# Buffers, stage places and PSUM banks in the scan part of a decoder layer: three decay half-sets, a gate every four chunks, three places a step

## The chip, the core and the metric

The kernel runs on one core of one Trainium2 chip. The metric is device time in microseconds, from the start to the end of one launch; a time is a median of several runs. Five engines work beside each other, each with its own queue of instructions: TensorE (PE in the profile; PEld is its weight load), VectorE (DVE), ScalarE (ACT), GpSimd (POOL) and SyncE (SP), which here only starts DMAs.

## The reference

The layer takes x and a context, both 8 x 256 x 256 (batch, sequence, width), and does three things in turn, each followed by a residual sum and a layernorm without gain.

A Mamba block: a projection to 2 x 512 channels, a causal convolution over 4 positions with silu, projections to a step size (softplus), B and C, and then the recurrence over 256 positions with 16 states for each of the 512 channels:

```
h = h * exp(d_t * A) + (d_t * u_t) * b_t
y = sum over the 16 states of h * c_t
y = (y + u * D_param) * silu(z)
out = y @ out_proj_w.T
```

A cross attention of one head to the context (keys and values are the same), whose result is normed and given to a feed-forward part of width 1024 with relu, and normed again.

A mixture of experts: 160 experts, the 8 best of each token by sigmoid, each expert a silu layer of width 128, and one shared expert.

## The kernel before

The program has a front (the Mamba block, the attention, the feed-forward part and the routing) and a back (the experts, from L768 on). The change is in the front only.

The front's recurrence goes over 128 steps: 8 batches b of 16 chunks n. A chunk is 32 channels by 16 states, laid on 128 partitions (32 channels by 4 states) and NG = 4 groups of 256 positions. One step n does this:

- `product` (L375): GpSimd multiplies the rows of B with step size times u into g, 128 x 1024. It is made LEAD = 3 steps ahead.
- `decays` (L381): ScalarE makes exp(d * A), 4 activations of 256 positions, into `decay`, two tiles of two groups in PSUM. They are written for the next step, behind the scans that read them.
- `scans` (L388): VectorE runs the recurrence as two scans of 2 x 256, one for each half-set.
- `read_out` (L397): VectorE multiplies the states with the rows of C into h.
- every fourth step `summed` (L412): TensorE adds up 16 states for 4 chunks into `ya`, 32 matmuls.

Beside this run two chains, Python generators that hand out one stage at each `yield`. `head(b + 1)` (L261) makes projections, convolution, silu, step size and the DMAs that spread them, for the next batch. `rest(b - 1)` (L423) does the previous batch's out projection, norm, attention, feed-forward part, norms and routing up to the places of its tokens; `scatter` (L660) then writes these to a table by indirect DMAs. `go` (L671) runs the first chain of a list to its next yield. For TensorE, VectorE, ScalarE and GpSimd the order in which the program issues instructions is the order of their queues (`manual_schedule`, L682), so an instruction that waits holds up all that stands behind it on its engine. SP's order is left to the planner.

In the kernel before, rest and head each get a stage in the middle of a step (behind the decays) and one at its end (behind read_out). If two rests are in the list, up to two more stages of the first are run at each of these. Head begins at n = 2 and is run to its end at n = NC - 6 = 10. Rest begins at the end of n = 0 of the next batch. Its second stage multiplies all of `ya` with silu(z) (L434), and needs `ya` of the whole batch, two PSUM tiles. `skipped` (L403) starts `ya` with u * D_param at n = 2.

The other matmuls of rest and head write to one pool of two PSUM tiles in turn (`bank`, L133; `ps_front`). A tile is given again when its readers are done.

When the last step is done, what is left of rest 6 and all of rest 7 run alone: the tail. Then come the counts of tokens, the gathering of token blocks and the experts' blocks.

Names that the steps of the prediction use: pj and pz (L266, L292) are the head's projections, L285 the convolution, L303 and L304 the silus, px and pd the projections to step size, L333 to L347 the softplus; po (L437), pk, pv and pq (L464, L472, L484), psc (L492), pat and pm (L517, L527) are the attention's banks; L538 makes x2, x2t (L546) is its turned form, ph and pf (L556, L568) are the feed-forward matmuls with relu (L567) between them, L576 adds their sum; L603 is the sigmoid, L613 the search for the 8 best, L638 to L644 the places, L650 to L656 the weights.

Of the kernel before, what the change touches and what calls it, by code (L numbers as in the profile page):

```python
# [9 lines left out]
F32 = mybir.dt.float32  # L10
AF = mybir.ActivationFunctionType
# [56 lines left out]
def decoder_layer(  # L68
# [109 lines left out]
    with ExitStack() as first:  # L178
# [3 lines left out]
        m3 = first.enter_context(tc.tile_pool(name="m3", bufs=PAIRS))  # L182
        m4 = first.enter_context(tc.tile_pool(name="m4", bufs=4))
        m5 = first.enter_context(tc.tile_pool(name="m5", bufs=5))
        pools["ps"] = first.enter_context(tc.tile_pool(name="ps_front", bufs=2, space=PSUM))
        acc = first.enter_context(tc.tile_pool(name="acc_front", bufs=2, space=PSUM))
# [64 lines left out]
        decay = [held.tile([P, 2, S], F32, name=f"decay{j}") for j in range(NG // 2)]  # L251
# [3 lines left out]
        states_f = states.rearrange("p g t -> p (g t)")  # L255

# [4 lines left out]
        def head(b, made):  # L261

            u = m1.tile([P, KI, S], F32, tag="u", name=f"u_{b}")
            sz = m2.tile([P, KI, S], F32, tag="sz", name=f"sz_{b}")
            for j in range(KI // 2):
                pj = bank(f"pj_{b}_{j}").rearrange("p (e t) -> p e t", e=2)  # L266
                for e in range(2):
                    o = (2 * j + e) * P
                    for k in range(KD):
                        nc.tensor.matmul(  # L270
                            pj[:, e, :], in_x[:, k, o : o + P], xt[:, k, :], start=(k == 0), stop=(k == KD - 1)
                        )
                yield
# [7 lines left out]
                for e in range(2):  # L281
                    k = 2 * j + e
                    for i in range(NTAP - 1):
# [5 lines left out]
                    if e == 0:  # L289
                        yield  # L290
            for j in range(KI // 2):
                pz = bank(f"pz_{b}_{j}").rearrange("p (e t) -> p e t", e=2)  # L292
                for e in range(2):
                    o = (2 * j + e) * P
                    for k in range(KD):
                        nc.tensor.matmul(
                            pz[:, e, :], in_z[:, k, o : o + P], xt[:, k, :], start=(k == 0), stop=(k == KD - 1)
                        )
                yield
                nc.scalar.copy(sz[:, 2 * j : 2 * j + 2, :], pz)  # L300
# [4 lines left out]
            exps()  # L305
            px = bank(f"px_{b}")
# [31 lines left out]
            yield  # L338
            nc.vector.scalar_tensor_tensor(e, delta, 1.0, e, ALU.subtract, ALU.subtract)
# [3 lines left out]
            exps()  # L343
            nc.gpsimd.tensor_sub(delta, delta, e)
            yield
# [16 lines left out]
        def spread(b, j, made):  # L362

            both = []
            for a, name in enumerate(("spread_delta", "spread_du")):
                t = m3.tile([P, 2, S], F32, tag=name, name=f"{name}_{b}_{j}")
# [14 lines left out]
        def decays(b, n, made):  # L381
            delta = made["spread"][n // 2][0]
            for g in range(NG):
                nc.scalar.activation(  # L384
                    decay[g // 2][:, g % 2, 1:], delta[:, n % 2, 1:], AF.Exp, scale=na[:, n * NG + g : n * NG + g + 1]
                )

        def scans(b, n, made):  # L388

            gf = made.pop(n)  # L390
            for j in range(NG // 2):
                part = slice(j * NT, (j + 1) * NT)
                nc.vector.tensor_tensor_scan(  # L393
                    states_f[:, part], decay[j].rearrange("p g t -> p (g t)"), gf[:, part], 0.0, ALU.mult, ALU.add
                )
# [7 lines left out]
        def skipped(b, made):  # L403

            made["ya"] = [acc.tile([P, NT], F32, tag="acc", name=f"ya_{b}_{j}") for j in range(KI // 2)]
            for k in range(KI):
                nc.tensor.matmul(
                    made["ya"][k // 2][:, (k % 2) * S : (k % 2 + 1) * S], diag[:, k, :], made["u"][:, k, :],
                    start=(k % 2 == 0), stop=False, skip_group_check=True,
                )  # L410

        def summed(b, k, made):  # L412


            hs = [made.pop(("h", k * NR + q)) for q in range(NR)]
            for g in range(NG):
                for q in range(NR):
                    nc.tensor.matmul(  # L418
                        made["ya"][k // 2][q * CH : (q + 1) * CH, (k % 2) * S : (k % 2 + 1) * S], over, hs[q][:, g, :],
# [3 lines left out]
        def rest(b, sz, ya):  # L423
# [7 lines left out]
            yield  # L431
            for j in range(KI // 2):
                g = sz[:, 2 * j : 2 * j + 2, :].rearrange("p k t -> p (k t)")
                nc.vector.tensor_mul(g, g, ya[j])  # L434
            yield

            po = bank(f"po_{b}").rearrange("p (c d) -> p c d", c=TT)  # L437
            for c in range(TT):
                for k in range(KI):
# [3 lines left out]
                    )  # L443
            yield
# [18 lines left out]

            pk = projected(wk, ct, "kt")  # L464
            yield
            nc.vector.tensor_add(xn, xn, po)
            kt = biased(early[:, 0], pk, C_BK)
            x1 = a1.tile([P, TT, D], F32, tag="x1", name=f"x1_{b}")
            layernorm(x1, xn, f"x1_{b}")
# [9 lines left out]
            nc.scalar.copy(val, pv)  # L479
            pt = turned(x1, f"x1_{b}")  # L480
            yield
            x1t = a1.tile([P, KD, S], F32, tag="x1t", name=f"x1t_{b}")
            nc.scalar.copy(x1t, pt)
            pq = projected(wq, x1t, "qt")  # L484
            yield
            qt = biased(early[:, 1], pq, C_BQ)
# [4 lines left out]
            nc.gpsimd.tensor_add(x1, x1, mid(rv[:, R_H2 : R_H2 + D], TT))  # L491
# [578 lines left out]
```

## Time and profile before

| | us |
| --- | --- |
| median of 11 runs | 1540.67 |
| lowest, highest | 1539.25, 1546.86 |
| the profiled execution | 1543.89 |
| its span, first to last instruction | 1542.2 |
| first scan | 51.62 |
| 128 steps | 51.6 to 850 |
| tail of the front | 850 to 943 |
| the rest, experts included | 943 to 1542.2 |
| mean granted TensorE clock | 0.803 |

A group's line gives busy time, the mean of one, and the idle time of its engine just before it with what ended that. A wait's line gives the total, how often, and the longest. A stretch's line gives its bounds and length, the busy time of PE, PEld, DVE, ACT and POOL with the number of instructions, the granted clock of TensorE, the DMA engines' share and GB/s. An order-of-time line gives start, length, engine, line, operation, operands and the count that was merged, with the idle time before it in brackets. The largest groups of the steps, of one step each: a scan of 128 x 512 1.229 us (L393), a product 2.354 (L378), one decay activation 0.474 (L384), a read_out 1.220 (L400). GpSimd's and VectorE's other work lies between these.

### The profile page before, as it was taken

How to read it: one execution, taken by the hardware profiler on the slowest of the kernel's cores; microseconds unless marked ns; L12 is line 12 of the kernel's file. 1: busy time of each engine (PE TensorE's matmuls, PEld its weight loads, DVE VectorE, ACT ScalarE, POOL GpSimd, SP SyncE). 2: the span in 40 equal slices, each digit the busy share in tenths (PEclk: the TensorE clock that was granted, in tenths of full speed). 3: DMA queues.
4: the chain of work that ended last, by engine and by line, in shares of the span. 5: the costliest groups of instructions: out<-in, count | busy, mean ns of one | idle time of the engine just before them, and what ended most of it. 6: DMA issues, size and time to landing. Idle time of an engine off the chain costs nothing. (4 is left out here: it accounts for less than half of the span.)

```text
span 1542.2 us, 18276 instructions
## 1 busy us (share of the span) xinstructions
PE 1004.5 (65%) x4831; PEld 703.3 (46%) x4831; DVE 880.0 (57%) x1776; ACT 667.6 (43%) x1540; POOL 883.0 (57%) x713
## 2 busy tenths in 40 slices
PE   4345757667657657575666661078888888877675
PEld 3223435345434534453444441056666666644333
DVE  2578778778768777887888317089433333310000
ACT  4264664854846647748546230022222222212222
POOL 1546374775756657747766014565656666637775
PEclk8576876878869868768778875579999999987877
DMA  6334752242343332323320000066867788634443
GB/s 206 109 95 121 236 176 64 53 108 50 56 96 63 65 83 61 101 64 48 110 53 2 21 7 7 3 190 198 239 198 219 212 228 249 196 115 132 132 133 93
DMA packets 159985, 177.13 MB, mean 115 GB/s; under 512 B 29220, under 2 KB 135238, under 8 KB 159872
## 3 DMA queue, kind: packets, MB, share of 16 engines
q1 hardware_dynamic: 127360, 131.31, 30.8%
q0 software_dynamic: 20704, 33.81, 8.3%
q10 hardware_dynamic: 11808, 10.75, 2.1%
q8 instruction: 42, 0.69, 0.2%
q14 instruction: 71, 0.58, 0.2%
HBM read 160.54 MB, written 51.97 MB: 138 GB/s over the span
## 5 line engine op out<-in xcount | busy, mean ns | idle before, releaser
L378 POOL TENSOR_TENSOR g<-bc,spread_du 128x1024 f32<-128x1024 f32 x128 | 300.2, 2354 | 118.2 <-DVE states L393 72.8
L393 DVE TENSOR_TENSOR_SCAN states<-decay,g 128x512 f32<-128x512 f32 x256 | 314.5, 1229 | 63.0 <-ACT decay L384 30.5
L384 ACT ACTIVATE decay<-spread_delta,na 128x255 f32<-128x255 f32 x512 | 238.5, 474 | 183.3 <-DVE states L393 153.2
L884 POOL DMA_INDIRECT xg<-x_d,tokens x216 | 215.9, 999 | 131.7 <-PE bt L895 122.1
L897 DVE COPY bx<-bt 128x256 f32<-128x256 f32 x216 | 91.5, 423 | 180.2 <-PE bt L895 178.4
L906 PE MATMUL by<-we,bg 128*128 128x256 f32 x432 | 151.4, 433 | 43.7 <-ACT bg L904 36.0
L904 ACT ACTIVATE bg<-bh 128x128 f32<-128x128 f32 x216 | 60.0, 278 | 246.9 <-PE bh L900 246.7
L400 DVE TENSOR_TENSOR h<-states,bc 128x1024 f32<-128x1024 f32 x128 | 156.1, 1220 | 9.5 <-PE ya L418 3.8
L988 POOL DMA_INDIRECT y<-y_d,sloti x128 | 121.0, 946 | 58.2 <-issue 55.1
L664 POOL DMA_INDIRECT tab_d<-pair_no,placei x128 | 125.7, 982 | 46.0 <-issue 30.2
L900 PEld LDWEIGHTS bh<-bx,we 128*128 128x128 f32 x864 | 129.9, 193 | 20.5 <-DVE bx L897 8.1
L900 PE MATMUL bh<-bx,we 128*128 128x128 f32 x864 | 134.6, 279 | 4.3 <-DVE bx L897 2.8
L994 PE MATMUL yn<-y,diags 128*128 128x256 f32 x256 | 108.1, 537 | 43.8 <-DMA y<-y_d,sloti 43.0
L906 PEld LDWEIGHTS by<-we,bg 128*128 128x128 f32 x432 | 65.4, 189 | 95.9 <-ACT bg L904 95.4
L418 PE MATMUL ya<-h,over 128*32 128x256 f32 x1024 | 87.6, 466 | 30.2 <-DVE h L400 30.2
L560 PE MATMUL ph<-x2t,w_sb 128*128 128x256 f32 x256 | 73.7, 458 | 47.8 <-ACT x2t L548 47.8
L171 PE MATMUL pt_x<-ident,x 128*128 128x128 f32 x96 | 26.4, 381 | 115.0 <-ACT x L162 99.1
L994 PEld LDWEIGHTS yn<-y,diags 128*128 128x128 f32 x256 | 55.8, 253 | 94.2 <-DMA y<-y_d,sloti 88.8
L995 DVE TENSOR_TENSOR xs<-xs,yn 128x512 f32<-128x512 f32 x8 | 5.5, 688 | 157.4 <-PE yn L994 157.4
L560 PEld LDWEIGHTS ph<-x2t,w_sb 128*128 128x128 f32 x256 | 59.5, 236 | 61.3 <-ACT x2t L548 50.4
L895 PE MATMUL bt<-ident,xg 128*128 128x128 f32 x432 | 83.6, 275 | 3.7 <-DMA xg<-x_d,tokens 3.7
L171 PEld LDWEIGHTS pt_x<-ident,x 128*128 128x128 f32 x96 | 14.0, 178 | 130.3 <-ACT x L162 111.5
(224 smaller groups left out, 1734.7 us busy)
## 6 DMA issues: line engine op xcount, KB each, us to landing
we<-in_experts_dram SPq DMA_DIRECT2D x216, 256.0 KB, 4.7
y_d<-bo SPq DMA_DIRECT2D x216, 128.0 KB, 3.2
spread_delta<-spread_d SPq DMA_DIRECT2D x256, 64.0 KB, 2.1
spread_du<-spread_d SPq DMA_DIRECT2D x256, 64.0 KB, 1.9
y_d<-none ACTq DMA_DIRECT2D x1, 9216.0 KB
bc<-bc_d SPq DMA_DIRECT2D x64, 128.0 KB, 4.7
spread_d<-delta SPq DMA_DIRECT2D x8, 512.0 KB
spread_d<-v SPq DMA_DIRECT2D x8, 512.0 KB
```

What stands on the lines that cost most here:

```text
L378: nc.gpsimd.tensor_mul(g, made["bc"][0], mid(made["spread"][n // 2][1][:, n % 2, :], NG))
L384: nc.scalar.activation(decay[g // 2][:, g % 2, 1:], delta[:, n % 2, 1:], AF.Exp, scale=na[:, n * NG + g : n * NG + g + 1])
L393: nc.vector.tensor_tensor_scan(states_f[:, part], decay[j].rearrange("p g t -> p (g t)"), gf[:, part], 0.0, ALU.mult, ALU.add)
L400: nc.vector.tensor_mul(h, states, made["bc"][1])
L560: nc.tensor.matmul(ph[:, i, :], w1_sb[:, k, f * P : (f + 1) * P], x2t[:, k, :], start=(k == 0), stop=(k == KD - 1),)
L664: nc.gpsimd.indirect_dma_start(out=tab_views[i * TOPK + j], out_offset=bass.IndirectOffsetOnAxis(ap=placei[:, c, j : j + 1], axis=0), in_= ...
L884: nc.gpsimd.indirect_dma_start(out=xg[i % LANES], out_offset=None, in_=x3_d, in_offset=bass.IndirectOffsetOnAxis(ap=tokens[:, i : i + 1], ...
L897: nc.vector.tensor_copy(xt, pt)
L900: nc.tensor.matmul(ph, w[:, k * P : (k + 1) * P], xt[:, k * P : (k + 1) * P], start=(k == 0), stop=(k == KD - 1))
L906: nc.tensor.matmul(py, g, w[:, KD * P :], start=True, stop=True)
L988: nc.gpsimd.indirect_dma_start(out=y8[:, j, :], out_offset=None, in_=y_d, in_offset=bass.IndirectOffsetOnAxis(ap=sloti[:, i, j : j + 1], a ...
L994: nc.tensor.matmul(pn[:, c, :], diags[:, i, j, :], y8[:, j, :], start=False, stop=(j == TOPK - 1))
```

## The change

- `decay` becomes three tiles (half-sets) instead of two; half-set j of step i uses tile (2 i + j) mod 3. `decays` and `scans` are called for one half-set. The first half for step i + 1 is written ahead of step i's scans, the second half behind them.
- A step has three places for rest: between the scans, behind the second scan (and the decays), behind read_out. With two rests in the list a place runs two stages. Head gets a stage at the second and third place, and one between the scans at even n.
- `ya` is one held PSUM tile of two 256-wide halves. `summed` begins a half with the product of u and D_param itself, and `gated` multiplies it with silu(z) one step later, at n = 1, 5, 9, 13. `skipped` is gone. Rest begins with po, at the last place of n = 1, and its three loads (`fetched`) are issued at n = 0.
- Rest and head have one PSUM tile each (`ps_rest`, `ps_head`) instead of two shared ones.
- Head begins at n = 0; the run to its end stands at the start of n = 10.
- More yields lie between an instruction and those that need its result, in rest and head. In rest, the norm of x1 comes ahead of pk.
- u has two buffers instead of one, silu(z) three instead of two; the g buffers stay four, under another name of the pool.

```diff
-        m3 = first.enter_context(tc.tile_pool(name="m3", bufs=PAIRS))
-        m4 = first.enter_context(tc.tile_pool(name="m4", bufs=4))
+        m3 = first.enter_context(tc.tile_pool(name="m3", bufs=3))
+        m4 = first.enter_context(tc.tile_pool(name="m4", bufs=PAIRS))
-        pools["ps"] = first.enter_context(tc.tile_pool(name="ps_front", bufs=2, space=PSUM))
-        acc = first.enter_context(tc.tile_pool(name="acc_front", bufs=2, space=PSUM))
+        pools["ps"] = first.enter_context(tc.tile_pool(name="ps_rest", bufs=1, space=PSUM))
+        ps_head = first.enter_context(tc.tile_pool(name="ps_head", bufs=1, space=PSUM))
...
-        decay = [held.tile([P, 2, S], F32, name=f"decay{j}") for j in range(NG // 2)]
+        decay = [held.tile([P, NG // 2, S], F32, name=f"decay{j}") for j in range(3)]
+        ya = held.tile([P, 2, S], F32, name="ya")
...
-            u = m1.tile([P, KI, S], F32, tag="u", name=f"u_{b}")
-            sz = m2.tile([P, KI, S], F32, tag="sz", name=f"sz_{b}")
+            u = m2.tile([P, KI, S], F32, tag="u", name=f"u_{b}")
+            sz = m3.tile([P, KI, S], F32, tag="sz", name=f"sz_{b}")
...
                 for e in range(2):
                     k = 2 * j + e
+                    yield
                     for i in range(NTAP - 1):
...
-                    if e == 0:
-                        yield
...
             exps()
+            yield
             px = bank(f"px_{b}")
...
             nc.scalar.activation(delta, delta, AF.Ln)
             exps()
+            yield
             nc.gpsimd.tensor_sub(delta, delta, e)
+            yield
             yield
             yield
...
-        def decays(b, n, made):
+        def decays(i, b, n, made, j):
+
             delta = made["spread"][n // 2][0]
-            for g in range(NG):
+            for e in range(NG // 2):
+                g = j * (NG // 2) + e
                 nc.scalar.activation(
-                    decay[g // 2][:, g % 2, 1:], delta[:, n % 2, 1:], AF.Exp, scale=na[:, n * NG + g : n * NG + g + 1]
+                    decay[(2 * i + j) % 3][:, e, 1:], delta[:, n % 2, 1:], AF.Exp,
+                    scale=na[:, n * NG + g : n * NG + g + 1],
                 )
...
         def summed(b, k, made):
+            nc.tensor.matmul(
+                ya[:, k % 2, :], diag[:, k, :], made["u"][:, k, :], start=True, stop=False, skip_group_check=True
+            )
...
-        def rest(b, sz, ya):
+        def gated(k, made):
+            nc.vector.tensor_mul(made["sz"][:, k, :], made["sz"][:, k, :], ya[:, k % 2, :])
+
+        def fetched(b):
...
+            return xn, ct, cn
+
+        def rest(b, sz, xn, ct, cn):
...
             yield
+            yield
...
-            pk = projected(wk, ct, "kt")
-            yield
             nc.vector.tensor_add(xn, xn, po)
-            kt = biased(early[:, 0], pk, C_BK)
             x1 = a1.tile([P, TT, D], F32, tag="x1", name=f"x1_{b}")
             layernorm(x1, xn, f"x1_{b}")
+            yield
+            pk = projected(wk, ct, "kt")
+            yield
+            yield
+            kt = biased(early[:, 0], pk, C_BK)
...
                     nc.scalar.activation(ht[:, f, :], ph[:, i, :], AF.Relu, bias=cv[:, C_B1 + f : C_B1 + f + 1])
+            yield
             pf = bank(f"pf_{b}").rearrange("p (c d) -> p c d", c=TT)
...
             for i, (b, n) in enumerate(steps):
...
-                scans(b, n, made)
+                if n == 0:
+                    if b + 1 < B:
+                        heads.append(head(b + 1, rows_made[b + 1]))
+                    if b > 0:
+                        begins = fetched(b - 1)
+                if n == 10:
+                    while heads:
+                        go(heads)
+                if after:
+                    decays(i + 1, *steps[i + 1], after_made, 0)
+                scans(i, b, n, made, 0)
                 while ahead < min(i + LEAD + 1, len(steps)) and ahead // 2 < loaded:
                     product(*steps[ahead], rows_made[steps[ahead][0]])
                     ahead += 1
-                if i + 1 < len(steps):
-                    decays(*steps[i + 1], rows_made[steps[i + 1][0]])
-                go(rests)
-                for _ in range(2):
-                    if len(rests) > 1:
-                        go(rests)
...
+                beside(rests)
+                if n % 2 == 0:
+                    go(heads)
+                scans(i, b, n, made, 1)
+                if after:
+                    decays(i + 1, *steps[i + 1], after_made, 1)
+                beside(rests)
+
                 if n % NR == 0 and i > 0:
                     b0, n0 = steps[i - 1]
                     summed(b0, n0 // NR, rows_made[b0])
                 go(heads)
                 read_out(b, n, made)
...
+                made.pop(n)
+                if n % NR == 1 and i > 1:
+                    b0, n0 = steps[i - 2]
+                    gated(n0 // NR, rows_made[b0])
+                    if n == 1:
+                        rests.append(rest(b0, rows_made[b0]["sz"], *begins))
+                beside(rests)
                 go(heads)
...
                 go(scattered)
```

`beside` runs one stage of the first rest, and a second one if two are in the list.

## The prediction

> **What bounds the kernel now.** I read the page first (busy shares and the 40 slices), then the stretches, then VectorE's waits, then the order of time of one batch.
>
> ```profile
> PE 1004.5 (65%) x4831; PEld 703.3 (46%) x4831; DVE 880.0 (57%) x1776; ACT 667.6 (43%) x1540; POOL 883.0 (57%) x713
> ...
> DVE  2578778778768777887888317089433333310000
> ACT  4264664854846647748546230022222222212222
> ```
>
> No engine is full. In slices 2 to 22, where the 128 scan steps run, VectorE is the fullest; the change touches only this part and what comes just before and after it. The stretches of five like batches, of the last batch, of the tail behind the last step, and of the rest:
>
> ```profile
> 234.80:763.80 529.00, 343.71 (x1740) 243.29 (x1740) 411.65 (x576) 332.33 (x711) 337.38 (x216) 0.78 0.33 73
> 759.80:850.00 90.20, 60.45 (x307) 42.04 (x311) 73.93 (x102) 50.01 (x120) 54.17 (x38) 0.75 0.15 37
> 850.00:943.00 93.00, 53.79 (x215) 39.52 (x212) 29.43 (x138) 25.66 (x62) 18.01 (x27) 0.74 0.05 14
> 943.00:1542.20 599.20, 429.12 (x2041) 303.64 (x2041) 209.18 (x785) 130.97 (x402) 365.90 (x374) 0.86 0.56 163
> ```
>
> 529.0 / 5 = 105.8 us a batch, of which VectorE (third pair) works 82.3. Some 4 us are the gaps between its instructions, so about 19 us a batch are waits. They are spread over many causes:
>
> ```profile
> DVE states L393 <- ACT decay L384: 30.5, 16, 3.6
> DVE best L613 <- ACT pr L603: 21.2, 7, 5.9
> DVE e L339 <- ACT delta L336: 15.2, 7, 2.5
> DVE delta L347 <- POOL delta L344: 13.3, 7, 4.2
> ...
> DVE x L576 <- PE pf L571: 11.3, 7, 2.3
> DVE den L628 <- ACT den L620: 10.6, 7, 1.7
> ```
>
> All of them over the 128 steps (without 11.8 at the start) are about 142 us: the most that the change can take away. A step with nothing else is short: scans at 635.26 and at 639.29, 4.0 us apart.
>
> ```profile
> 635.26 2.57 DVE L393 TENSOR_TENSOR_SCAN states<-decay,g 128x512 f32<-128x512 f32 x2
> 637.94 1.23 DVE L400 TENSOR_TENSOR h<-states,bc 128x1024 f32<-128x1024 f32 x1
> 639.29 2.57 DVE L393 TENSOR_TENSOR_SCAN states<-decay,g 128x512 f32<-128x512 f32 x2
> 643.39 0.69 DVE L576 TENSOR_TENSOR x<-x,pf 128x512 f32<-128x512 f32 x1 [1.53 <-PE pf L571]
> ```
>
> The last line is the join that will matter: VectorE reaches the FFN's sum and waits 1.53 for TensorE, which had been busy with it since 627.23:
>
> ```profile
> 627.23 8.93 PE L560 MATMUL ph<-x2t,w_sb 128*128 128x256 f32 x32 [7.25 <-ACT x2t L548]
> 636.18 7.17 PE L571 MATMUL pf<-w_sb,ht 128*128 128x256 f32 x32
> 643.28 1.93 PE L418 MATMUL ya<-h,over 128*32 128x256 f32 x32
> ```
>
> **Where the stages come to stand.** Counting yields, rest grows from 39 stages to 51, head from 17 to 23. With three places a step (A between the scans, B behind the second, C behind read_out), from the third batch on: xn's sum stands at step 2 C, x2's at 9 B, x2t at 10 B, ph 0 to 3 at 10 C to 11 C, pf's halves at 12 B and 12 C, the FFN's sum at 13 B, sigmoid at 16 A (step 0 of the next batch), the top 8 at 1 A, places and weights at 2 A. The head: convolutions at steps 1 to 3, the two silus at 4 between the scans, exp at 6, the logarithm at 7, the end at 8.
>
> **What goes.** decays for a first half waits for a scan one and a half steps back, so the plain decay wait goes. sigmoid has a whole step before the top 8 (-3.0 a batch, 21.2 / 7), den, exp and u get distance (-1.5, -2.2, -1.4).
>
> **What comes.** I follow one batch round: VectorE, then ScalarE, then TensorE, each handing over to the next.
>
> Segment 1, VectorE, from the FFN's sum (13 B) to the last convolution (step 3): 0.7 + 1.05 (norm statistics) + 1.25 (read_out) + 0.45 (a gate of 256; the 256-wide sum at L693 took 0.42) = 3.45; step 14 is 4.0 + 1.05 + 0.4 wait for POOL's two sums; steps 15 and 0 are 4.0 each; step 1 is 4.0 + 2.2 (top 8) + 0.2 + 3.0 (two convolutions of 1.5) + 0.45; step 2 is 4.0 + 3.0 (places, 2.5 to 3.6 in the trace) + 1.9 (weights) + 1.75 + 1.5; step 3 up to its convolution is 2.6 + 1.5. Sum 43.0.
>
> Segment 2. The head has one bank, so pz waits for the last convolution: 2.0, copy 0.6, second pz 2.0, copy 0.6, hops 0.1: 5.3. Then ScalarE is nearly without a pause up to x2t: table, silu, silu, table 4.7; 13 half-sets of decays at 0.95 (two of 0.474) = 12.4; x1t, val, xd, prob_t and at 2.8; v twice and qt 2.6; abs, exp and the 1+ 3.3; top and softmax 1.5; logarithm with two tables 3.7; x2's norm 2.1; x2t 1.0: 34.1 in all, with about 5 of waits, of which 2.9 is for x2's sum that waits for pm. With the 5.3: 44.4. Inside it VectorE meets the second half-set of step 5, which stands behind the silus: from the last convolution to that decay's end 5.3 + 4.7 + 0.95 = 11, VectorE needs 1.25 + 4.0 + 1.3 = 6.5: a wait of 4.5 in place of the 3.6 seen now. At steps 7 and 9 it waits another 2 and 1.4.
>
> Segment 3. After x2t the first ph takes 3.75 (the trace has 627.23 to 631.02, granted clock 0.52 up to 631 and 1.00 after); with one bank each next ph waits for the relu before: 3 x 1.75, and 4 x (0.84 + hops) = 3.6; pf's halves 3.6 each; summed, which now stands between them with its own diagonal product, 1.93 + 0.47. Sum 22.2, where before the same stretch took 16.1. VectorE has 0.65 of step 10, steps 11 and 12 and two scans to do: 11.2. So it waits 11 us, partly for step 13's decays behind the relus.
>
> Round: 43.0 + 44.4 + 22.2 = 109.6, 3.8 more than 105.8. Both ends: the first ph at full clock -2, half of ScalarE's 5 us of waits gone -2.5: 105.1; pz at the low clock, as at 84.59 where it took 3.65, +1.65, and 2 for VectorE and POOL slowing each other (L640 has a mean of 1.2 against 0.17 alone): 113. I take 109.6, since the last batch and the tail show ph after a pause at the low clock each time.
>
> The other parts: batches 2 to 6, 5 x 3.8 = +19. Batch 1 (95.3 now) has no top 8, places or weights; by the same round without 4.1 + 3.0 of these it comes to 102: +6.5. Batch 0 (83.9): 8.6 for the first step, 77 for the rest with a 4.5 to 6 wait at the silus: +2. Batch 7 (90.2), where the head is missing but segment 3 is whole: 91, +1. The first head runs alone: its second pj and first pz wait for convolutions instead of a second bank, 20.0 to 26.5 at the silus' start, +6.5. The tail: po no longer waits for the places (-5.5), but pk and pv share a bank (+4.2) and so do the ph (+3.5): +2. Asking for xn, ct and cn a step earlier costs nothing: 0.4 us each on SP's queue, which stands idle from 571.9 to 576.35 in the batch read here. The head's DMAs move two steps forward with it, so the next batch's spreads are asked for at step 10 instead of 11; VectorE waits for no DMA in a steady batch, so this hides behind four pairs loaded ahead, and without these it would cost up to the 2 us that one transfer takes. On POOL steps 7 to 9 now hold three products, the head's two products and three scatters, 3 x 2.36 + 2 x 2.35 + 3 x 2.5 = 19.3 against some 19 of VectorE's; the three products made ahead cover it, and without them each us beyond would be VectorE's. The experts' part (599 us) is not touched. Sum +37. The profiled execution took 1543.89, its span 1542.2 and 1.7 around it; the median is 3.2 lower. I put the sum on the median: 1540.7 + 37 = **1578**.
>
> **Two rules of the Trainium skill.** On one bank instead of two, the trace has relus 1.73 apart with two banks, and 1.75 + 0.9 is the round with one. "TensorE: Matmul & The Clock Gate", section "HAM oscillation", tells of a kernel in which a second PSUM buffer gave no further gain; by it the second bank's loss would cost nothing, 2.7 a batch less, and the sum would be about 1559; no run here has shown it yet, and that kernel had no relu between.
> The trace has a silu starting 0.01 us after its 1.28 us table (601.42, 602.71). "ScalarE: Activation LUTs", section "What ACT_TABLE_LOAD costs", adds a drain of about 1.38 to each load; by it the silus would hold ScalarE 2.8 longer in each of 7 batches and the sum would be near 1597. The row decides.
>
> **Rivals.**
> (a) Slower, as summed: 1553 to 1600 (the ends of the round over five batches, 3 us for the rest). Chance 0.50.
> (b) Faster: the FFN's distance suffices, and the wait at 13 B stays 1.5 as now. Then 9.5 us in each of 7 batches are not lost: 1578 - 66 = 1512. For it: TensorE worked 343.7 of 529 us, so it has room. Against it: steps 10 to 12 carry nothing else for VectorE, so three of them are only 12 us. It decides from a wait of 11 - 37 / 7 = 5.7 downwards. Chance 0.27, 1490 (with 3 us a batch of the other waits gone too) to 1537.
> (c) The waits only change places: rounds of 105.8 and only the start, batch 1 and the tail pay: about 1541 + 10 = 1551 down to no change. Chance 0.14, a quarter of it within 0.2%.
> (d) TensorE, pausing after each ph, stays at half clock: ph 3.6 and pf 7.2 each, +12 in 7 batches: 1662. For it 0.52 at 627; against it, full-rate groups after 0.7 us pauses in the tail (pq at 877.29, 8 in 1.99). Chance 0.09.
>
> **How the numbers follow.** (a)'s own range is 1553 to 1600. Leaving out (d) and the lower third of (b), together under 0.2, gives 1506 to 1605. A change of 0.2% (3 us) is about what a measurement of this kernel can tell. Faster 0.27 + a little of (c) = 0.28, same 0.04, slower 0.68.
>
> **What would show it.** VectorE's wait list led by the FFN's sum on pf (near 9 a batch), then scans on decays at the second half of step 5 (about 4.5); best, den and e near none; ph in groups with pauses of 0.9; first scan near 58 instead of 51.6. If the wait on pf is below 5.7, or ScalarE shows pauses between the silus and x2t of much over 5, the sum is wrong.

## The result and the profile after

The changed kernel takes 1624.5 us (median of 8 runs, 1620.31 to 1628.67) against 1541.54 for the kernel before (31 runs): a ratio of 1.0532, 95% interval 1.0516 to 1.0548. The forecast said slower, by 37 us, and 1506 to 1605 as the range; the kernel is slower by 83, above the range's upper end.

The page's busy line and slices of the kernel after (the span is 1621.4 us in place of 1542.2):

```profile
PE 1056.3 (65%) x4831; PEld 721.2 (44%) x4831; DVE 873.4 (54%) x1793; ACT 660.6 (41%) x1540; POOL 882.4 (54%) x713
...
DVE  1469579759757867777598411629733333320000
ACT  2364565745845755647455322002222222222221
```

VectorE, ScalarE and GpSimd are busy for about as long as before (880.0, 667.6, 883.0 then). Only TensorE is busy for longer, 1056.3 in place of 1004.5, with the same 4831 recorded matmuls: these took longer on the mean. The added time is waiting, and part of the waiting is for slower matmuls. The stretches of the 128 steps, of the tail up to the routing's matmul (pl, L616) and of the rest (bounds and length, busy time of PE, PEld, DVE, ACT and POOL, granted clock, DMA share, GB/s), first before, then after (there the steps stand last):

```profile
51.60:850.00 798.40, 504.25 (x2531) 348.58 (x2535) 631.54 (x829) 490.93 (x1050) 489.20 (x297) 0.77 0.34 85
850.00:924.90 74.90, 47.06 (x198) 35.02 (x195) 14.81 (x55) 23.18 (x58) 8.78 (x9) 0.80 0.04 14
924.90:1542.20 617.30, 435.85 (x2059) 308.14 (x2059) 223.79 (x866) 133.45 (x406) 375.14 (x391) 0.85 0.54 159
```

```profile
915.00:1004.80 89.80, 58.83 (x199) 39.65 (x198) 13.88 (x53) 22.12 (x57) 8.82 (x9) 0.69 0.03 9
1004.80:1621.40 616.60, 436.87 (x2060) 306.38 (x2059) 223.68 (x866) 133.40 (x406) 375.22 (x391) 0.85 0.54 159
62.60:915.00 852.40, 536.73 (x2519) 360.17 (x2519) 626.00 (x847) 484.18 (x1048) 488.44 (x297) 0.76 0.34 80
```

The back part is unchanged (616.6 against 617.3). In the tail the clock granted to TensorE fell from 0.80 to 0.69. By place, against the forecast (batch times are from a batch's first scan to the next one's):

| place | before | after | measured | forecast |
| --- | --- | --- | --- | --- |
| up to the first scan | 51.6 | 62.6 | +11.0 | +6.5 |
| batch 0 | 83.9 | 89.4 | +5.5 | +2 |
| batch 1 | 95.3 | 105.8 | +10.5 | +6.5 |
| batches 2 to 6 | 529.0 | 565.9 | +36.9 | +19 |
| batch 7 | 90.2 | 91.3 | +1.1 | +1 |
| last step to pl | 73.4 | 88.5 | +15.1 | +2 |
| sum | | | +80.1 | +37 |

VectorE's waits over the 128 steps of the kernel after (total, how often, the longest):

```profile
DVE states L403 <- ACT decay L395: 99.7, 35, 7.9
DVE x L594 <- PE pf L589: 51.3, 7, 7.7
...
DVE top L515 <- PE psc L508: 9.8, 7, 8.0
...
DVE den L649 <- ACT den L640: 0.4, 1, 0.4
```

The joins are those of the forecast. The waits for best and e are no longer in the list, den is at 0.4, and decays (30.5 before) and pf (11.3 before) lead. Decays come first and pf second, the other way round than forecast. Order of time of the worst decay wait of a batch, on TensorE, ScalarE and VectorE:

```profile
513.11 3.11 PE L278 MATMUL pz<-xt,in_z 128*128 128x256 f32 x8 [2.75 <-DVE u L298]
516.90 3.78 PE L278 MATMUL pz<-xt,in_z 128*128 128x256 f32 x8 [0.68 <-ACT sz L305]
...
520.71 0.59 ACT L305 COPY sz<-pz 128x512 f32<-128x512 f32 x1 [2.98 <-PE pz L278]
521.32 1.28 ACT L308 ACT_TABLE_LOAD   x1
522.61 1.06 ACT L308 ACTIVATE u<-u 128x1024 f32<-128x1024 f32 x1
523.57 1.04 ACT L309 ACTIVATE sz<-sz 128x1024 f32<-128x1024 f32 x1
524.64 1.28 ACT L138 ACT_TABLE_LOAD   x1
525.93 0.99 ACT L395 ACTIVATE decay<-spread_delta,na 128x255 f32<-128x255 f32 x2
...
526.95 1.23 DVE L403 TENSOR_TENSOR_SCAN states<-decay,g 128x512 f32<-128x512 f32 x1 [7.56 <-ACT decay L395]
```

The first pz waits for the convolution that reads the head's one tile, the second for the copy of the first; they take 3.11 and 3.78 at a granted clock of 0.59 and 0.51; a like group takes 1.99 at 1.00 elsewhere. This is batch 4. In batches 2 to 6 the first pz takes 3.11 to 3.49, the second 3.78 or 3.76 in two of them and 1.99 in three. ScalarE stands in pz's copies, the silus stand behind these, and behind the silus stands the half-set that VectorE needs. And the join of the feed-forward part in the same batch, on TensorE and VectorE:

```profile
561.17 3.78 PE L577 MATMUL ph<-x2t,w_sb 128*128 128x256 f32 x8 [1.81 <-ACT x2t L564]
565.88 1.99 PE L577 MATMUL ph<-x2t,w_sb 128*128 128x256 f32 x8 [0.93 <-ACT ht L584]
568.80 1.99 PE L577 MATMUL ph<-x2t,w_sb 128*128 128x256 f32 x8 [0.93 <-ACT ht L584]
571.72 1.99 PE L577 MATMUL ph<-x2t,w_sb 128*128 128x256 f32 x8 [0.93 <-ACT ht L584]
574.65 3.72 PE L589 MATMUL pf<-w_sb,ht 128*128 128x256 f32 x16 [0.93 <-ACT ht L584]
578.21 0.59 PE L417 MATMUL ya<-u,diag 128*128 128x256 f32 x2
578.73 1.93 PE L423 MATMUL ya<-h,over 128*32 128x256 f32 x32
580.59 3.72 PE L589 MATMUL pf<-w_sb,ht 128*128 128x256 f32 x16
...
584.42 0.69 DVE L594 TENSOR_TENSOR x<-x,pf 128x512 f32<-128x512 f32 x1 [7.69 <-PE pf L589]
```

Four pauses of 0.93 for the relu that reads rest's one tile, as forecast; 23.25 from the first ph to the sum. The granted clock is 0.50 over the first ph and 1.00 over the others. In other batches it stays low for longer. The same four groups in batch 2:

```profile
333.75 3.78 PE L577 MATMUL ph<-x2t,w_sb 128*128 128x256 f32 x8 [1.81 <-ACT x2t L564]
338.46 3.78 PE L577 MATMUL ph<-x2t,w_sb 128*128 128x256 f32 x8 [0.93 <-ACT ht L584]
343.17 3.63 PE L577 MATMUL ph<-x2t,w_sb 128*128 128x256 f32 x8 [0.93 <-ACT ht L584]
347.73 1.99 PE L577 MATMUL ph<-x2t,w_sb 128*128 128x256 f32 x8 [0.93 <-ACT ht L584]
```

Here the sum comes 26.68 after the first ph. Of batches 2 to 6, the second ph is slow in three and the third in two.

### The profile page after: what moved, and what is told of

It is laid out like the page before. It is cut to its first block, busy times and chain, and to the rows that moved or that the text cites. A ratio compares the mean times of both kernels' runs of the same rounds, so it can differ in the third digit from the quotient of the medians.

```text
span 1621.4 us, 18259 instructions
## 1 busy us (share of the span) xinstructions
PE 1056.3 (65%) x4831; PEld 721.2 (44%) x4831; DVE 873.4 (54%) x1793; ACT 660.6 (41%) x1540; POOL 882.4 (54%) x713
## 5 line engine op out<-in xcount | busy, mean ns | idle before, releaser
L403 DVE TENSOR_TENSOR_SCAN states<-decay,g 128x512 f32<-128x512 f32 x256 | 314.6, 1229 | 135.1 <-ACT decay L395 99.7
L685 POOL DMA_INDIRECT tab_d<-pair_no,placei x128 | 130.1, 1016 | 49.6 <-issue 28.7
L1022 POOL DMA_INDIRECT y<-y_d,sloti x128 | 121.1, 946 | 58.4 <-issue 56.0
L934 PEld LDWEIGHTS bh<-bx,we 128*128 128x128 f32 x864 | 129.9, 193 | 20.2 <-DVE bx L931 8.1
L577 PE MATMUL ph<-x2t,w_sb 128*128 128x256 f32 x256 | 88.1, 504 | 36.5 <-ACT ht L584 22.3
L423 PE MATMUL ya<-h,over 128*32 128x256 f32 x1024 | 77.0, 428 | 16.9 <-DVE h L411 16.9
L597 POOL TENSOR_TENSOR x<-x,rv 128x512 f32<-128x512 f32 x8 | 10.1, 1263 | 140.1 <-ACT x L162 140.1
```

The source lines that it names most:

```text
L403: nc.vector.tensor_tensor_scan(states_f[:, part], decay[(2 * i + j) % 3].rearrange("p g t -> p (g t)"), made[n][:, part], 0.0, ALU.mult, A ...
L577: nc.tensor.matmul(ph[:, i, :], w1_sb[:, k, f * P : (f + 1) * P], x2t[:, k, :], start=(k == 0), stop=(k == KD - 1),)
L685: nc.gpsimd.indirect_dma_start(out=tab_views[i * TOPK + j], out_offset=bass.IndirectOffsetOnAxis(ap=placei[:, c, j : j + 1], axis=0), in_= ...
L934: nc.tensor.matmul(ph, w[:, k * P : (k + 1) * P], xt[:, k * P : (k + 1) * P], start=(k == 0), stop=(k == KD - 1))
L1022: nc.gpsimd.indirect_dma_start(out=y8[:, j, :], out_offset=None, in_=y_d, in_offset=bass.IndirectOffsetOnAxis(ap=sloti[:, i, j : j + 1], a ...
```

## The experiments

The experiments were run in three groups, each on another chip: the kernel before had 1566.62 in the first (one to four), 1535.77 in the second (five to eight), 1566.51 in the third (nine to twelve). Ratios are taken within a group; beside them stands the time in the profile at which the routing's matmul of the last batch starts (pl: before 923.44, after 1003.45), which leaves out the experts' part. The chips differ in that part: from pl on it takes 634 to 651 us in the profiles of the first and third groups, 615 to 617 in those of the second and 618 in that of the kernel after. The times that the expectations of the first group name are those of the result's chip; by the ratio the kernel after would take some 1650 in that group.

**1. Shared tiles.** Only the PSUM pools are put back: one pool of two tiles for rest and head.

```diff
-        pools["ps"] = first.enter_context(tc.tile_pool(name="ps_rest", bufs=1, space=PSUM))
-        ps_head = first.enter_context(tc.tile_pool(name="ps_head", bufs=1, space=PSUM))
+        pools["ps"] = first.enter_context(tc.tile_pool(name="ps_front", bufs=2, space=PSUM))
...
-            def bank(name):
-                return ps_head.tile([P, NT], F32, tag="ps_head", name=name)
```

> The changed kernel with one thing undone: rest and head take their PSUM tiles from one pool of two, as before the change, instead of one each. Theory B (a bank for each chain makes each chain wait for its own last reader): the first scan goes back from 62.6 to about 52, the tail behind the last step from 88 to about 75, the FFN's stretch from x2t's end to the FFN's sum from 23.3 to about 18 and pz's from 6 to 3, so some 6 us in each of 7 batches; in all 60 to 70 less than 1624.5, 1555 to 1565. Theory P (the places of the stages set the waits, not the banks): only start and tail come back, 1595 to 1605, and VectorE still waits over 6 us a batch for pf.

Ratio 1.0009 [0.998, 1.0038]; pl at 916.20. The whole loss is gone. Against the kernel after, the first scan comes at 50.5 instead of 62.6 (-12.1), the steps take 793.8 instead of 852.4 (-58.6), and last step to pl 71.9 instead of 88.5 (-16.6): together 87. By the ratios it is 5.2%, some 81. The feed-forward join of this kernel in batch 4, order of time on TensorE:

```profile
514.92 8.75 PE L573 MATMUL ph<-x2t,w_sb 128*128 128x256 f32 x32 [1.36 <-ACT x2t L560]
523.50 3.62 PE L585 MATMUL pf<-w_sb,ht 128*128 128x256 f32 x16
...
529.34 3.72 PE L585 MATMUL pf<-w_sb,ht 128*128 128x256 f32 x16
```

Here ph has no pauses, and first ph to sum is 18.25 (514.92 to 533.17), 5.0 less. The two pz with their last copy take 5.9 (470.50 to 476.42) instead of 8.2 (513.11 to 521.30). A batch of 2 to 6 is shorter by 7.8 (527.0 against 565.9 for the five). On the mean of these batches 6.6 of it lie between x2t's end and the sum (18.4 instead of 25.0), and 1.2 between the last convolution and x2t's end (45.4 instead of 46.6): the feed-forward join is most of it.

**2. The head's silus behind the second half-set.** In the kernel after, head's stage between the scans moves behind the second decays (one execution).

```diff
                 beside(rests)
-                if n % 2 == 0:
-                    go(heads)
                 scans(i, b, n, made, 1)
                 if after:
                     decays(i + 1, *steps[i + 1], after_made, 1)
+                if n % 2 == 0:
+                    go(heads)
```

> The changed kernel with the head's extra stage of even steps moved from between the scans to behind the second half-set's decays, so that step 5's second decays no longer stand behind the silus. Theory P: the wait of 7.6 at that decay goes and VectorE gains most of it in 7 batches, 30 to 45 less, 1580 to 1595. Theory A (ScalarE's whole stretch from the silus to x2t is what a batch waits for, so a wait that goes there comes back further on): the waits on decays fall by half, those on psc, pm and pf grow by as much, and the time stays within 10 of 1624.

1651.41, 1.054 of before; pl at 999.98, 3.5 earlier. The waits for decays fell from 99.7 to 68.6, but others took their place: top 9.8 to 15.6, x2's sum on pm 16.1 to 20.7, and h on ya (14.4) and total (9.1) are new in the list. The list fits ScalarE being held for as long, with the next instructions late instead; what each of them waited behind was not followed.

**3. The feed-forward sum later.** Three more empty stages ahead of it, in the kernel after (one execution).

```diff
+            yield
+            yield
+            yield
             yield
             nc.vector.tensor_add(x2, x2, pf)
```

> The changed kernel with three more empty stages ahead of the FFN's sum, which so stands at step 14 instead of 13. Theory P: the 7.3 us a batch that VectorE waits for pf are covered by one more step of scans: 20 to 30 less (4.0 a batch), 1595 to 1605. Theory A, read strictly (the round of a batch is a closed chain through the sum): the wait falls by 4, and the places and the po of the same rest come a step later; if these are not on the round it gains the same 4.0 a batch, if they are, nothing: 1624.

1653.99, 1.056; pl at 1001.65. VectorE's waits in the steps:

```profile
DVE states L403 <- ACT decay L395: 88.0, 33, 7.8
DVE h L411 <- PE ya L423: 49.4, 11, 8.6
...
DVE x L597 <- PE pf L589: 6.6, 6, 1.8
```

The wait on pf went from 51.3 to 6.6, and h on ya came up with 49.4: the sums of step 12 now stand behind the third or fourth ph on TensorE (in one batch at 580.57, behind a ph that began at 576.52), and read_out of step 13 waits up to 8.6 to overwrite h, which they read. The same lateness, met at another instruction.

**4. The old distances.** The kernel after without its 19 added yields: 38 stages of rest and 17 of head, at three places a step (one execution).

```diff
             for j in range(KI // 2):
                 pj = projected(in_x, j, "pj")
                 yield
...
                 for e in range(2):
                     k = 2 * j + e
-                    yield
...
+                    if e == 0:
+                        yield
...
                     nc.scalar.activation(ht[:, f, :], ph[:, i, :], AF.Relu, bias=cv[:, C_B1 + f : C_B1 + f + 1])
-            yield
             pf = bank(f"pf_{b}").rearrange("p (c d) -> p c d", c=TT)
```

> The changed kernel with the yields of before in rest and head (38 and 17 stages instead of 51 and 23), all else as changed: what the longer distances alone are worth. If the distances help, as the counts of sigmoid and top 8 say (waits on best, e, den and u were 7 us a batch before and are near 1 now), it is slower than 1624.5, near 1650. If the three places a step crowd the chains and the distances only keep them apart in name (theory A: ScalarE's and TensorE's chain is what counts), it is within 15 of 1624.

1748.22, 1.116; pl at 1112.58, 109 later than in the kernel after. One execution gives the size only roughly, but the sign is plain: at three places a step the old number of stages brings the user of each result closer to it, and the added yields are needed to make up for that.

**5. Two half-sets.** Shared tiles as in the first, and only two decay tiles, each half written behind its scan.

```diff
-        decay = [held.tile([P, NG // 2, S], F32, name=f"decay{j}") for j in range(3)]
+        decay = [held.tile([P, NG // 2, S], F32, name=f"decay{j}") for j in range(2)]
...
-                    decay[(2 * i + j) % 3][:, e, 1:], delta[:, n % 2, 1:], AF.Exp,
+                    decay[j][:, e, 1:], delta[:, n % 2, 1:], AF.Exp,
...
+                scans(i, b, n, made, 0)
                 if after:
                     decays(i + 1, *steps[i + 1], after_made, 0)
-                scans(i, b, n, made, 0)
```

> The changed kernel with one shared pool of two tiles (as in e1_shared) and, besides, two decay half-sets instead of three, each written behind the scan that reads it. Theory H (three half-sets give ScalarE a step of room): waits of the scans on decays come back, 3 to 4 us a batch more, about 25 to 30 over e1_shared's ratio of 1.001, so 1.015 to 1.02 of before. Theory A (ScalarE's stretch sets the round, with or without room): within 0.5% of e1_shared, 0.997 to 1.006.

Ratio 1.0132 [1.0111, 1.0152]; pl at 937. Against the first experiment, which is of another group, the third half-set is worth 1.2% with two shared tiles: less than theory H's 1.015 to 1.02, more than theory A allows. VectorE's waits for decays are 69.0 here and 56.9 there.

**6. TensorE kept busy in the tail.** In the kernel after, one more matmul into the idle `ya` behind every stage of the last rest; the result is not used (one execution).

```diff
                 go(rests)
+                if len(rests) == 1:
+                    nc.tensor.matmul(ya[:, 0, :], ident, rv[:, :S], start=True, stop=True, skip_group_check=True)
```

> The changed kernel with one extra matmul of 128 x 256 behind every stage of the tail (the last rest alone), into a PSUM tile that nothing reads any more; nothing is left out. It fills TensorE's pauses there. Theory C (a good part of the tail's loss is the low clock that the pauses bring): the groups pq, psc, pat and the second ph go from 3.78 to near 2.0 and the stretch from po's start to the routing's first matmul from 74.9 to 67 to 71, in spite of 0.4 more work a stage. Theory W (the waits for the one bank alone): the groups stay at 3.78 or the extra work eats the gain: 75 to 85.

1608.83, 1.048; pl at 991.81. Order of time on TensorE, first the kernel after:

```profile
944.74 3.78 PE L459 MATMUL pqt<-x1t,attn_w 128*128 128x256 f32 x8 [0.68 <-ACT x1t L494]
949.45 3.78 PE L508 MATMUL psc<-early 128*128 128x256 f32 x8 [0.93 <-ACT early L469]
...
957.09 3.78 PE L535 MATMUL pat<-prob_t,early 128*128 128x256 f32 x8 [0.67 <-ACT prob_t L530]
...
969.55 3.78 PE L577 MATMUL ph<-x2t,w_sb 128*128 128x256 f32 x8 [1.11 <-ACT x2t L564]
974.26 3.78 PE L577 MATMUL ph<-x2t,w_sb 128*128 128x256 f32 x8 [0.93 <-ACT ht L584]
```

and the same groups with the added matmuls:

```profile
940.36 1.97 PE L459 MATMUL pqt<-x1t,attn_w 128*128 128x256 f32 x8
942.16 1.03 PE L799 MATMUL ya<-rv,ident 128*128 128x256 f32 x4
943.26 1.99 PE L508 MATMUL psc<-early 128*128 128x256 f32 x8
...
948.68 1.97 PE L535 MATMUL pat<-prob_t,early 128*128 128x256 f32 x8
...
959.47 2.75 PE L577 MATMUL ph<-x2t,w_sb 128*128 128x256 f32 x8
962.06 0.59 PE L799 MATMUL ya<-rv,ident 128*128 128x256 f32 x2
963.15 1.99 PE L577 MATMUL ph<-x2t,w_sb 128*128 128x256 f32 x8 [0.50 <-ACT ht L584]
```

More work, and the tail is shorter: from po to pl 66.3 (925.52 to 991.81) in place of 74.9 (928.60 to 1003.45); before it took 57.7 (865.73 to 923.44), and with two shared tiles (the first experiment) 58.4. The granted clock over this stretch is 0.71 in the kernel after, 0.89 with the added matmuls and 0.83 before. So of the 17.1 us that it lost against before, at least 8.6 come with the low clock. The 8.6 that remain hold the pauses for the single tile and the time of the added matmuls; these two were not told apart.

**7. Later places for pf.** Shared tiles as in the first; pf's halves stand behind the sums of step 12 and their sum at step 14, by three more yields.

```diff
+            yield
             pf = bank(f"pf_{b}").rearrange("p (c d) -> p c d", c=TT)
...
+            yield
+            yield
             yield
             nc.vector.tensor_add(x2, x2, pf)
```

> e1_shared, with pf's halves put behind the sums of step 12 and the FFN's sum at step 14 instead of 13 (three more empty stages). e1_shared waits 6.1 us a batch for pf; one more step of scans covers 4.0 of it. Theory P: 20 to 28 less than e1_shared, 0.983 to 0.990 of before. Theory A (closed round): the wait moves to another join, within 0.5% of e1_shared.

Ratio 0.9988 [0.9968, 1.0008]; pl at 917.77. The wait on pf is nearly gone in the steps (42.9 in the first experiment, 3.3 here), and the time is the same within 0.5%: waits for decays (56.9 there, 71.3 here), of top on psc (8.5 and 18.9) and of h on ya (not in the list there, 20.2 here) took its place.

**8. Three shared tiles.** Two half-sets as in the fifth, the bank set free given to the pool, and the later places of the seventh. The pool's line against the seventh's:

```diff
-        pools["ps"] = first.enter_context(tc.tile_pool(name="ps_front", bufs=2, space=PSUM))
+        pools["ps"] = first.enter_context(tc.tile_pool(name="ps_front", bufs=3, space=PSUM))
```

> Two decay half-sets, and the tile that this frees goes to the shared pool, which has three; pf and the FFN's sum as in e7_late. If a third tile for the chains is worth more than the third half-set: below e7_late by 0.5% or more. If two tiles already take away the banks' waits, as e1_shared's start (50.5) and tail suggest: as e7_late plus what e5_two loses against e1_shared.

1519.4, ratio 0.9903 [0.988, 0.9926]; pl at 901.28. This is 1% faster than the kernel before, and so faster than both kernels. VectorE's waits in its steps:

```profile
DVE states L399 <- ACT decay L391: 55.8, 31, 4.6
DVE h L407 <- PE ya L419: 22.9, 10, 3.6
DVE top L511 <- PE psc L504: 12.7, 6, 3.1
...
DVE x L593 <- PE pf L586: 3.3, 3, 1.8
```

No decay wait is over 4.6 (7.9 in the kernel after).

**9 and 10. The same three banks, divided.** Two half-sets as in the fifth; of the three tiles rest has two and head one, and the other way round. The first of them against the fifth's kernel:

```diff
-        pools["ps"] = first.enter_context(tc.tile_pool(name="ps_front", bufs=2, space=PSUM))
+        pools["ps"] = first.enter_context(tc.tile_pool(name="ps_rest", bufs=2, space=PSUM))
+        ps_head = first.enter_context(tc.tile_pool(name="ps_head", bufs=1, space=PSUM))
...
+            def bank(name):
+                return ps_head.tile([P, NT], F32, tag="ps_head", name=name)
```

> Two half-sets of decays, so that a bank is free; rest has two PSUM tiles of its own, head one. Beside it stands the kernel with the same two half-sets and two shared tiles, at 1.0132 times before. Theory R (rest carries the loss: pauses between its groups in the feed-forward part, 6 us a round in segment 3, and in the tail, 16): only the head's share stays, the start at +11 (first scan near 60) and about 2 us a round from the second pz behind the convolution: 11 + 7 x 2 = 25 us, 1.03 at most, less what rest gains by never sharing. Theory H (the head's single tile carries it, since its pz stands in front of the silus and all of ScalarE's queue behind them): 1.04 to 1.06.

> The same with one tile for rest and two for head. Theory R: the tail at +16, segment 3 at +6 a round in seven rounds: 1.0132 + 58/1536 = 1.05; the first scan back near 49. Theory H: near 1.01 to 1.02. If both kernels stay near 1.03, the loss is shared by both chains.

Head with one tile: 1.028 [1.0257, 1.0303]. Rest with one tile: 1.0395 [1.0365, 1.0425]. Both chains carry part of the loss, rest more. The places are roughly as expected. With two shared tiles (the fifth) the first scan comes at 48.60 and a batch of 2 to 6 takes 108.1 on the mean. With one tile for head these are 64.46 and 109.5; with one tile for rest 53.07 and 112.4, and the last step's end to pl is some 15 longer.

**11 and 12. What three tiles and the distances are worth.** The fifth with three shared tiles; and the same without the 19 added yields.

> Two half-sets and a shared pool of three tiles, without the later places of pf and of its sum. If the third tile alone makes the kernel faster than before, 0.990 to 0.995 (the later places were worth 0.2% with two tiles); if it only pays together with the later places, because the wait on pf (6.5 a batch) hides the gain, 1.005 to 1.013.

> As the kernel with three shared tiles and two half-sets, with the fewer stages of before (38 and 17 yields' worth). If the longer distances are worth by themselves what they were worth in the changed kernel (1748 against 1651, 6%): 1.04 to 1.06. If they only paid there for waits on the single tiles: within 1% of the kernel with three tiles and the longer distances.

Three shared tiles: 1.001 [0.9989, 1.0031], pl at 912.56. With nine and ten this is the plainest comparison: three banks in one pool 1.001, divided two and one 1.028, one and two 1.0395. Against two shared tiles (1.0132, another group) the third is worth 1.2%. The later places of pf then bring another 1.1% (to 0.9903 in the eighth, again another group), where with two tiles they brought 0.2%; so neither expectation holds whole.

Without the added yields: 1.0558 [1.0524, 1.0592], pl at 1026.93. The distances are worth 5.5% also where no chain waits for a single tile. VectorE's waits in its steps:

```profile
DVE top L503 <- PE psc L496: 51.6, 7, 11.7
DVE x L577 <- PE pf L572: 39.5, 7, 5.6
```

## Why the prediction was wrong

**The step that failed** is the price of one PSUM tile for each chain, a term that was in the sum and too small. It stood at four places (ph, pz, the start, the tail), with the right mechanism at each: a group waits for the last reader of the one before. Where the prediction names a price it is 2.7 in each of seven batches for ph, 6.5 at the start and 7.7 in the tail, some 33 in all; pz has none of its own. The runs show that this one part is the whole loss (undone, 1.0009), and its price is 81 us by the ratios and 87 by the places of the first experiment. Most of what was missing is one thing: groups behind these waits run at a low clock where the sum had full clock. Its terms, in turn:

- The round. Over batches 2 to 6 the three segments measure 41.8, 46.6 and 25.0 on the mean, some 113 together, where 43.0, 44.4 and 22.2 were forecast, 109.6 together. Segment 3, from x2t's end to the sum, is the furthest off. It took 23.3 in the two batches where the first ph ran at half clock and three at full, as forecast, and 25.1 to 26.8 in the three where the second ph, and in two of them the third, ran slow too. In segment 2 the pz stretch was put at 5.3 with both groups at full clock and took 7.3 on the mean. The slow groups that were not forecast make 2.0 a batch at pz and 1.7 at ph. The upper end of 113 held the low clock for one pz, 1.65; its row (3.65 at 84.59) was nearer to the rule than to an end.
- The start, forecast +6.5, measured +11.0. The tile's wait was seen for the second pj and the first pz; but each such group followed a pause of some 4 us and took 3.75 and 3.38 instead of about 2.0, which is 3.1 of the 4.5 missing; and pd, on one tile too, was left out and takes 1.5 more.
- The tail, forecast +2, measured +15.1. pk with pv and the ph were put at +4.2 and +3.5, 7.7 together; with most groups back at full clock the sixth experiment leaves a loss of 8.6. Not seen was that pq, psc, pat and two of the ph then run at 3.78 instead of 1.99, five times 1.79; the added matmuls took 8.6 off. And po starts 2.0 earlier after the last step (13.7 against 15.7), not 5.5.
- Batches 0 and 1, forecast +8.5, measured +16.0. With the tiles shared they take 80.3 and 99.7 instead of 89.4 and 105.8, so the tile is 15.2 here. In batch 0 only the head runs beside the steps: its second pj and its first pz each wait 7.04 for a convolution and take 3.75, and VectorE's wait at the silus is 7.89 where 4.5 to 6 was forecast.

**Rival (d)**, half clock after each pause, had 0.09 and was partly what came: true in the start, at the first pz, for much of the tail, and in batches 2 to 6 for the second ph in three and the third in two; untrue for the fourth ph and for pf. The row cited against it, pq at 877.29 in 1.99 in the tail of before, came from a stretch in which po, pk and pv ran without a pause up to 874.86. In the kernel after pk and pv stand behind pauses of 0.78 and 1.88, and pq takes 3.78. A row from the kernel before does not hold for a place where the change itself takes away the work around it.

**Rival (b)**, that the feed-forward sum's distance suffices: fell. The wait at 13 B is 7.69, over the 5.7 at which it decides (the forecast put it at 11, partly at step 13's decays, where 3.32 and 1.64 are seen).

**Rival (c)**, that waits only change places, describes the kernel with the tiles shared: the waits for best, e and den are gone there, decays and pf wait longer, and the time is that of before. Decays there wait 56.9 in 37 waits (30.5 in 16 before), the longest 7.4. So the plain decay wait did not go, as the prediction had it: against two half-sets (69.0 in 49 waits, the fifth experiment) the third takes 12 off. The rival's price for the batches was right only for that kernel.

**What was right:** the sign; which waits of VectorE vanish (best, e, den) and which two lead, though not their order; the place of the worst decay wait (step 5's second half, forecast 4.5, measured 7.56, with the 2.9 of pz in the difference); the ph in groups with pauses of 0.9; the experts' part untouched. One reading of before was off, though no term of the sum rests on it: of the 21.2 that best waits for the sigmoid, 15.2 in six waits lie within the steps, and the longest, 5.9, behind the last one.

**The two rules of the Trainium skill.** The one of "TensorE: Matmul & The Clock Gate", section "HAM oscillation", that a second PSUM buffer gave no further gain, does not carry over: one tile for each chain instead of two shared costs 5.2% here (1.0532 against 1.0009). For the drain that "ScalarE: Activation LUTs", section "What ACT_TABLE_LOAD costs", adds to a load, the kernel after shows a silu at 522.61, 0.01 us after a load that ran from 521.32 for 1.28; no drain is seen.

**What stays open.** How much of the 36.9 us in batches 2 to 6 is the clock and how much the pauses was not tried; fillers were run in the tail only. The 3.7 a batch above is an estimate from the rows, and not all of it is the tile's: with two shared tiles the 32 recorded matmuls of ph, one stretch there, took 8.7 in three of these batches and 10.2 in two. What makes the second and third ph slow in one batch and not in the next is open as well.

## What to carry to other kernels

As far as these runs show, chains that run beside each other should draw from one PSUM pool: a pool of their own with one tile made each matmul group wait for the last reader, and three banks did better in one pool than divided. Price such a wait twice, once as the pause and once with the next groups at the low clock, wherever nothing else keeps TensorE busy. Moving the one instruction that shows a wait brought nothing here while the work behind it was as late as before (the third and seventh experiments); the wait showed again at another join. With a third shared tile the same move brought 1.1%.

## What the runs showed of the hardware that was not expected

A group of eight recorded 128x256 matmuls took 1.99 us at a granted clock of 1.00 and 3.78 at 0.50. In the tail with pauses of 0.67 to 1.11 between groups, five of them took 3.78; with matmuls of 0.59 to 1.9 us put into the pauses, four of these took 1.97 to 1.99, and the first ph 2.75. The length of one pause alone does not decide: behind the same pause of 0.93 the second ph ran in 1.99 in batch 4 and in 3.78 in batch 2, and in the tail pm ran in 1.99 behind a pause of 0.68 while pat just ahead of it, behind 0.67, took 3.78. What does decide was not tried.
